# A transformer block on one core: a rewritten order for the first hundred microseconds

## The chip, the cores and the metric

The kernel runs on one core of one Trainium2 chip. The core has five engines that run at the same time and wait for each other through semaphores: TensorE (PE; its weight loads are shown apart as PEld), VectorE (DVE), ScalarE (ACT), GpSimd (POOL) and SyncE (SP), which in this kernel issues nearly all DMAs. The metric is the device time of one execution in microseconds (us). Three runs of the kernel before took 2388.63, 2390.82 and 2393.79 us; the median is 2390.82.

## The reference

The input is four sequences of 4096 rows of 512 values. In order:

```python
x = x + 0.5 * ffn(layernorm(x), weight, bias)
x = x + attention(layernorm(x), qkv_w, qkv_b, rpb, proj_w, proj_b)
x = x + 0.5 * ffn(layernorm(x), weight, bias)
```

`ffn` is one matrix product of 512 by 512. Both operands are first rounded, in blocks of 32 along the inner dimension, to a six-bit floating-point grid with one scale for each block, and scaled back; so the weight, too, has to be quantised before the first product. `attention` has 16 heads of 32; every row sees 13 neighbours, with a bias by relative position, and is followed by an output projection.

## The kernel before, in words

The 16384 rows are 128 tiles of 128 rows; four tiles are a group. Every product is done in float16 with a high and a low half of each operand: `product` (L146) issues twelve matmuls for 512 output columns, low weight half first. All weights lie in one tile `wt`, as 2 halves x 4 chunks of the inner dimension x 2560 columns: 512 each for queries, keys, values and the output projection, and last the FFN weight, from column FO. A weight is worked on in its row layout, 128 rows at a time, and has to be transposed on its way into `wt`.

Work on a tile is cut into stages that run at numbered slots (`begin`, `run_slot`, L162 to L169): a stage issues some instructions, yields how many slots later and at what rank it goes on, and within a slot low ranks are issued first. One tile advances by STEP = 7 slots. Engines execute in the order of issue. The stages are:

- `load` (L174), `moments` and `quantised_norms` (L214, L220): statistics on VectorE, factors on POOL (`factors`, L183), the normalised tile on ScalarE, block maxima on VectorE, a product with the reciprocal on POOL, rounding to fp8 on ScalarE, a product with the scale on POOL, then the high half on ScalarE, the low half on VectorE (`low`, L202) and a DMA transpose into `xT`;
- `first_half` (L281): the FFN product `pmf` on TensorE, its addition to x (L279), the second norm, halves `hln`, and a DMA transpose into `x2`, which holds a group. `add_bias` puts half the FFN bias onto x on POOL (L568);
- `values` (L303): the product `pmv`, its halves `vt`, and a store `vd<-vt`;
- `project_qk` (L353): two products `pmqk` for one head group, which need all four tiles of the row group in `x2`. This is item m. `softmax` (L421) computes scores `ps`, VectorE, POOL and ScalarE work in turn, and transposes the probabilities by DMA, `pT<-p` (L489). `attend` (L492) multiplies with the stored values, which `load_stack` (L398) has loaded back, `vs<-vd`. Then come `project_out` and `second_half`, with the store of the result.

A tile t of k = 7t begins its FFN at slot k + 5 and its values at k + 20; the items begin at slot 38 and then every seven slots.

The setup block (L629 to L873) does three things. It loads the FFN weight `fw` and quantises it by exact steps in four row groups (L745 to L770): VectorE does most of the elementwise work (L752, L756 to L758, L142, L144), POOL the products with the two halves of the scale (L755) and the scaling back (L766), ScalarE the rounding (L762) and the high half (L768), and the sync queue transposes (`wt<-whlf`, L704). It finds powers of two for all weights from sums of squares (`powers`, L670). And it scales the other sixteen weight chunks (`put_scaled`, L781, halves `whl`, L784 and L786, then `wt<-whl`), at slots 2 to 35; `scales` (L795), `attention_bias` (L813, product `pmb`) and `put_table` (L858) belong here. From L779 the code is a written order (`manual_schedule`); what stands before it was put in order by a planner at build time, with its own estimates. The first three tiles are normed there too.

Buffers limit how far engines run apart: three PSUM buffers `ps_m` for products, 23 buffers `x` for tiles.

Of the kernel before, what the change touches and what calls it, by code (L numbers as in the profile page):

```python
# [26 lines left out]
F32 = mybir.dt.float32  # L27
# [10 lines left out]
P = 128  # L38
# [12 lines left out]
QB = 32  # L51
# [13 lines left out]
def macaron_kernel(  # L65
# [70 lines left out]
    def tie_to_lower(t):  # L136

        nc.vector.scalar_tensor_tensor(t, t, BELOW_ONE, t, ALU.mult, ALU.min)  # L142
        ti = t.bitcast(I32)
        nc.vector.tensor_scalar(ti, ti, 1, None, ALU.bitwise_or)  # L144

# [74 lines left out]
    def quantised_norms(slot):  # L220

        tiles, mv = together.pop(slot)
        n = len(tiles)
        rs, nb = factors(slot, "q", mv[0], n)
# [21 lines left out]
        nc.gpsimd.tensor_tensor(yb, yb, bc(r, QB), ALU.mult)  # L246
# [4 lines left out]
        nc.gpsimd.tensor_tensor(  # L251
# [3 lines left out]
        if spare:  # L255
            hl = xp.tile([P, dim], F32, tag="x", name=f"hlq{slot}").bitcast(F16)
            hl = hl.rearrange("p (u s k) -> p u s k", u=1, s=2)
        else:
            hl = hlp.tile([P, 2, 2, dim], F16, tag="hlq", name=f"hlq{slot}")[:, :n]
# [11 lines left out]
    def ffn(t, which):  # L271

        xT = ys.pop(t)
        pm = ps_m.tile([P, dim], F32, tag="mm", name=f"pm{which}_{t}")
        product(
            pm, lambda s, c: xT[:, s, c, :], lambda s, c: wt[:, s, c, FO : FO + dim]
        )
        yield 1, 8
        nc.vector.scalar_tensor_tensor(xs[t], pm, cf, xs[t], ALU.mult, ALU.add)  # L279

    def first_half(t):  # L281

        yield from ffn(t, "f1")
        yield 1, 2
        mv = sm.tile([P, 1, 2], F32, tag="mvn2", name=f"mvn2_{t}")
        statistics(t, "n2", mv[:, 0, :])
        yield 1, 2
        rs, nb = factors(t, "n2", mv)
        yield 1, 2
        y = yp.tile([P, 1, dim], F32, tag="yn2", bufs=1, name=f"yn2_{t}")  # L290
        nc.scalar.activation(y[:, 0], xs[t], AF.Identity, bias=nb, scale=rs)
        hl = hlp.tile([P, 1, 2, dim], F16, tag="hln2", name=f"hln2_{t}")
# [273 lines left out]

    def add_bias(t, b):
        nc.gpsimd.tensor_tensor(xs[t], xs[t], b, ALU.add)  # L568
# [30 lines left out]
    for t in range(NT):  # L599
        k = t * STEP  # L600
        begin(k - 18, one(load, t), 0)
        enlist(k - 10, t, "n1")
        if not 0 < t < EARLY:
            begin(k - 11, one(moments, k - 10, t, "n1"), 1)
        begin(k + F1, first_half(t))
        begin(k + V, values(t))
        begin(k + F1, one(add_bias, t, half_ffn_b), 8)
# [6 lines left out]
    for slot in together:  # L614
        if slot >= EARLY * STEP - 10:
# [13 lines left out]
    with tc.tile_pool(name="setup", bufs=1) as sp, tc.tile_pool(name="scratch", bufs=2) as scr:  # L629
# [10 lines left out]


        rows = {}

        sq = sp.tile([P, 5 * KC], F32, name="sq")
        first = min(slots)
        for slot in range(first, first + EARLY * STEP, STEP):
            run_slot(slot)
        for _ in quantised_norms(-10):
            pass
        chunks = (8, 9, 10, 11, 12, 13, 14, 15, 0, 4, 1, 5, 2, 6, 3, 7)  # L650
        for o in chunks:
# [3 lines left out]
        for o in (*range(4 * KC, 5 * KC), *chunks):  # L655
            src = fw[:, o - 4 * KC, :] if o >= 4 * KC else rows[o]
            junk = scr.tile([P, dim], BF16, tag="junk", name=f"junk{o}")
            nc.scalar.activation(junk, src, AF.Square, accum_out=sq[:, o : o + 1])
        ptb = ps_m.tile([P, 512], F32, tag="mm", name="ptb")
        nc.tensor.transpose(ptb[:, : 3 * KC], b12, ident[: 3 * KC, : 3 * KC])  # L660
        bT = sp.tile([P, 3 * KC], F32, name="bT")
        nc.vector.tensor_copy(bT, ptb[:, : 3 * KC])
        b2 = sp.tile([P, 3 * KC], F32, name="b2")
        nc.vector.scalar_tensor_tensor(b2, bT, 2.0 ** -8, bT, ALU.mult, ALU.mult)
        nc.vector.tensor_tensor(sq[:, : 3 * KC], sq[:, : 3 * KC], b2, ALU.add)
        top5 = sp.tile([P, 5], F32, name="top5")
        up = sp.tile([P, 5], F32, name="up")
        down = sp.tile([P, 5], F32, name="down")

        def powers(lo, hi):  # L670
# [7 lines left out]
            nc.tensor.transpose(ptn[:w, :P], top5[:, lo:hi], ident)  # L678
            most = sp.tile([w, 1], F32, name=f"most{lo}")
            nc.vector.tensor_reduce(most, ptn[:w, :P], AX.X, ALU.max)  # L680
            diag = sp.tile([w, w], F32, name=f"diag{lo}")
            nc.vector.tensor_scalar(diag, ident[:w, :w], most, 2.0, ALU.mult, ALU.mult)
            ones_w = sp.tile([w, P], F32, name=f"ones{lo}")
            nc.gpsimd.memset(ones_w, 1.0)
            pb = ps_m.tile([P, 512], F32, tag="mm", name=f"pb{lo}")
            nc.tensor.matmul(pb[:, :w], ones_w, diag, start=True, stop=True)
            e = sp.tile([P, w], I32, name=f"e{lo}")
            nc.vector.tensor_copy(e.bitcast(F32), pb[:, :w])
            nc.vector.tensor_scalar(e, e, 23, None, ALU.logical_shift_right)
            nc.vector.tensor_scalar(e, e, 131, None, ALU.add)  # L690
            nc.vector.tensor_scalar(e, e, 1, None, ALU.logical_shift_right)
            nc.vector.tensor_scalar(e, e, 97, None, ALU.max)
            u, d = up[:, lo:hi].bitcast(I32), down[:, lo:hi].bitcast(I32)
            nc.vector.tensor_scalar(u, e, -1, 264, ALU.mult, ALU.add)
            nc.vector.tensor_scalar(u, u, 23, None, ALU.logical_shift_left)
            nc.vector.tensor_scalar(d, e, -10, None, ALU.add)
            nc.vector.tensor_scalar(d, d, 23, None, ALU.logical_shift_left)

        powers(4, 5)
# [219 lines left out]
```

## Time and profile before

| | |
|---|---|
| median of three runs | 2390.82 us |
| the profiled execution | 2398.3 us, of them 2396.5 us span |
| TensorE busy | 2285.3 us (95%) |
| VectorE busy | 2020.8 us (84%) |
| GpSimd busy | 1990.2 us (83%) |
| ScalarE busy | 1329.8 us (55%) |
| first FFN product, first q/k projection | at 58.50 us, at 107.18 us |

The page of a profile gives busy times and shares of the span, 40 slices with the busy share in tenths, and the costliest groups of instructions. A line of a timeline reads: start in us, duration in us, engine, line, operation, output <- inputs, shapes, count, and in brackets the idle time of the engine before it and what ended it. "SPq" is the sync queue: its durations are the time of issuing a DMA, and the data land later. A group's mean can mix shapes.

### The profile page before, as it was taken

To read this page: it belongs to the slowest core of one execution; us is meant where nothing else is said; L and a number is where in the kernel's file an instruction comes from. 1 tells how busy PE (TensorE), PEld (TensorE's weight loads), DVE (VectorE), ACT (ScalarE), POOL (GpSimd) and SP (SyncE) were. 2 spreads that over 40 slices of the span, in tenths; PEclk is the share of its full clock that TensorE was granted. 3 is DMA by queue.
4 is the path that set the end of the run, shared out by engine and by line. 5 is a ranking of instruction groups with operands and counts; after the bars stand their busy time and mean duration, and the time that the engine had idled before them with its cause. 6 is when DMAs were issued, how large, how long until landed. Compare 5 with 4: busy or idle time off the path is not lost.

```text
span 2396.5 us, 82360 instructions
## 1 busy us (share of the span) xinstructions
PE 2285.3 (95%) x35539; PEld 1118.5 (47%) x35539; DVE 2020.8 (84%) x3588; ACT 1329.8 (55%) x2080; POOL 1990.2 (83%) x2012
## 2 busy tenths in 40 slices
PE   0799999999999999999999999999999999999998
PEld 0344444444444444444444444444444444444443
DVE  8789888888888888888888888888888878888886
ACT  4466555555555555555555555555555555555542
POOL 5578888888888888888888888888888888888886
PEclk9899999999999999999999999999999999999999
DMA  5789788777777777777777778877777786777773
GB/s 153 143 151 155 159 164 159 159 148 151 150 155 158 158 142 150 148 155 156 164 147 149 148 159 161 156 159 146 150 151 158 158 158 131 149 150 152 137 116 108
DMA packets 925701, 360.59 MB, mean 150 GB/s; under 512 B 718876, under 2 KB 889752, under 8 KB 925336
## 3 DMA queue, kind: packets, MB, share of 16 engines
q1 hardware_dynamic: 924992, 354.79, 74.3%
q8 instruction: 278, 4.55, 0.8%
q10 hardware_dynamic: 344, 0.53, 0.1%
q14 instruction: 87, 0.71, 0.1%
HBM read 110.15 MB, written 67.29 MB: 74 GB/s over the span
## 4 chain that ended last, share of the span: by engine, by line
PE 92%; DVE 4%; issue 1%; DMA 1%; POOL 1%; ACT 1%; SPq 0%; DVEq 0%; POOLq 0%; ACTq 0%
PE pmqk L151 28%; PE pmf L151 26%; PE pmo L151 14%; PE pmv L151 14%; PE ps L437 7%; PE pv L507 3%; DVE fw L756 0%; DMA x<-hln 0%; DVE hlq L204 0%; DVE stn L180 0%; DVE whl L786 0%; DMA fw<-in_L_ffn_weight_dram 0%; DVE sc L239 0%; POOL yq L251 0%; DVE x L279 0%
## 5 line engine op out<-in xcount | busy, mean ns | idle before, releaser
L151 PE MATMUL pmf<-wt,xT 128*128 128x512 f16 x3048 | 703.2, 381 | 12.9 <-DMA xT<-hlq 10.3
L151 PE MATMUL pmqk<-x,wt 128*128 128x512 f16 x3072 | 709.3, 381 | 4.8 <-DMA x<-hln 4.6
L151 PEld LDWEIGHTS <-xT 128*128 128x128 f16 x3048 | 298.8, 98 | 377.1 <-DMA xT<-hlq 12.7
L151 PEld LDWEIGHTS <-wt 128*128 128x128 f16 x3072 | 290.6, 98 | 342.7 <-issue 10.4
L151 PE MATMUL pmo<-wt,ring 128*128 128x512 f16 x1536 | 360.5, 385 | 8.5 <-issue 8.5
L151 PE MATMUL pmv<-wt,x 128*128 128x512 f16 x1536 | 354.1, 380 | 4.9 <-DVE mvn L181 4.9
L246 POOL TENSOR_TENSOR yq<-yq,r 128x1024 f32<-128x1024 f32 (+1 forms) x141 | 246.7, 1750 | 131.1 <-DVE r L244 131.1
L568 POOL TENSOR_TENSOR x<-x,half_ffn_b 128x512 f32<-128x512 f32 x256 | 327.8, 1280 | 0.1
L279 DVE SCALAR_TENSOR_TENSOR x<-pmf,coef,x 128x512 f32<-128x512 f32 x256 | 179.7, 702 | 151.9 <-PE pmf L151 151.6
L534 ACT ACTIVATE ring<-pv 128x510 f16<-128x510 f32 (+8 forms) x224 | 82.6, 415 | 396.6 <-PE pv L507 396.6
L314 ACT CAST vt<-pmv 128x512 f16<-128x512 f32 x128 | 75.1, 587 | 389.2 <-PE pmv L151 389.2
L180 DVE BATCH_NORM_STATS2 stn<-x 128x6 f32<-128x512 f32 x384 | 265.4, 691 | 9.0 <-DMA x<-in_L_attn_x_dram 0.2
L251 POOL TENSOR_TENSOR yq<-q,sc 128x1024 f32<-128x1024 fp8e4 (+1 forms) x141 | 246.9, 1751 | 1.0 <-ACT q L249 1.0
L151 PEld LDWEIGHTS <-x 128*128 128x128 f16 x1536 | 150.7, 98 | 187.6 <-DMA x<-hln 5.4
L377 DVE SCALAR_TENSOR_TENSOR qk<-pmqk,qk_b,qk 128x512 f16<-128x512 f32 x256 | 190.7, 745 | 52.9 <-ACT qk L373 51.8
L151 PEld LDWEIGHTS <-ring 128*128 128x128 f16 x1536 | 141.6, 99 | 173.2 <-issue 19.9
L480 POOL TENSOR_TENSOR sf<-sf,total 128x714 f32<-128x714 f32 (+2 forms) x128 | 178.8, 1397 | 42.8 <-DVE total L478 22.9
L186 POOL TENSOR_SCALAR rsq<-mv 128x2 f32<-128x2 f32 (+1 forms) x141 | 130.0, 922 | 99.3 <-DVE mv L181 96.9
L249 ACT ACTIVATE q<-yq,nudge 128x1024 fp8e4<-128x1024 f32 (+1 forms) x141 | 150.3, 1066 | 112.0 <-POOL yq L246 103.8
L373 ACT ACTIVATE qk<-pmqk,qk_b 128x512 f16<-128x512 f32 x256 | 176.5, 689 | 52.2 <-PE pmqk L151 50.4
L233 ACT ACTIVATE yq<-x,nbq,rsq 128x512 f32<-128x512 f32 x254 | 193.6, 806 | 18.3 <-POOL nbq L192 17.6
L487 POOL TENSOR_TENSOR p<-sf,p 128x714 f16<-128x714 f32 (+2 forms) x128 | 192.8, 1506 | 0.1
(145 smaller groups left out, 3466.3 us busy)
## 6 DMA issues: line engine op xcount, KB each, us to landing
vs<-vd SPq DMA_DIRECT2D x144, 357.0 KB
x<-in_L_attn_x_dram SPq DMA_DIRECT2D x128, 256.0 KB
vd<-vt SPq DMA_DIRECT2D x128, 256.0 KB
out_dram<-x SPq DMA_DIRECT2D x128, 256.0 KB
vs<-vd SPq DMA_DIRECT2D x24, 378.0 KB
vs<-vd SPq DMA_DIRECT2D x24, 315.0 KB
rows<-in_L_attn_qkv_w_dram SPq DMA_DIRECT2D x12, 256.0 KB
xT<-hlq SPq DMA_TRANSPOSE x141
```

What stands on the lines that cost most here:

```text
L151: nc.tensor.matmul(pm, lhs(a, c), rhs(b, c), start=(n == 0), stop=(n == 3 * KC - 1))
L180: nc.vector.bn_stats(st, xs[t])
L233: nc.scalar.activation(y[:, u], xs[t], AF.Identity, bias=nb[:, u : u + 1], scale=rs[:, u : u + 1])
L246: nc.gpsimd.tensor_tensor(yb, yb, bc(r, QB), ALU.mult)
L251: nc.gpsimd.tensor_tensor(yb, q8.rearrange("p u (n q) -> p (u n) q", q=QB), bc(sc, QB), ALU.mult)
L279: nc.vector.scalar_tensor_tensor(xs[t], pm, cf, xs[t], ALU.mult, ALU.add)
L373: nc.scalar.activation(t[:, s, 0, KN:], pms[s], AF.Identity, bias=bias)
L377: nc.vector.scalar_tensor_tensor(t[:, s, 1, KN:], pms[s], bias, t[:, s, 0, KN:], ALU.add, ALU.subtract)
L437: nc.tensor.matmul(ps[rows, u, :sides, w * KN : (w + 1) * KN], t[rows, 0, part, q0 : q0 + QR], t[rows, 1, :sides, k0 : k0 + KN], start=par ...
L480: nc.gpsimd.tensor_tensor(s, s, bc(total[:, :n], KN), ALU.mult)
L487: nc.gpsimd.tensor_tensor(p[:, :n, KN : 2 * KN], s, ph, ALU.subtract)
L568: nc.gpsimd.tensor_tensor(xs[t], xs[t], b, ALU.add)
```

## The change

It concerns the setup block and the slots of the first six tiles; from tile 6 on the stages are the same and stand at the same slots.

1. The written order now begins before the setup's work; the planner orders only what comes ahead of it (the first loads and constants). The order of the setup is written out with generators that are advanced step by step (`run`, `both`).
2. The FFN weight is quantised by VectorE alone apart from ScalarE's rounding: L755 and L766 move from POOL to VectorE. Row groups 0 and 1 are done first, then 2 and 3. The scaled-back weight is transposed by TensorE in 128 by 128 pieces into PSUM; ScalarE copies the high half into `wt` and VectorE subtracts for the low half. The DMA transposes of the FFN weight are gone. For the first two tiles, the two products of `quantised_norms` move to VectorE.
3. `begin_ffn` issues the first 256 columns of the FFN product of tiles 0 and 1, as soon as row groups 0 and 1 are in `wt`; `ffn` then issues the other 256.
4. The first six tiles get slots of their own for norm, FFN and values (N1, FIRST, VALUES), and `first_half` other waits between its steps.
5. The other weights: early chunks are loaded first; values come at slots 6 to 9, the first two items' queries and keys at 15 to 34, the rest at 42 to 51, the output projection at 56 to 67, where they stood at 2 to 35. The bias product moves from slot 28 to 70, the table from 26 to 31.

```diff
@@ quantised_norms
+        mult = nc.vector if slot in N1[:2] else nc.gpsimd
...
-        nc.gpsimd.tensor_tensor(yb, yb, bc(r, QB), ALU.mult)
+        mult.tensor_tensor(yb, yb, bc(r, QB), ALU.mult)
...
@@ ffn, first_half
+    def begin_ffn(t):
+
+        xT, n = ys[t], dim // 2
+        pm = ps_m.tile([P, dim], F32, tag="mm", name=f"pmf1_{t}")
+        product(pm[:, :n], lambda s, c: xT[:, s, c, :], lambda s, c: wt[:, s, c, FO : FO + n])
+        begun[t] = pm, n
...
+        if which == "f1" and t in begun:
+            pm, n = begun.pop(t)
+        else:
+            pm, n = ps_m.tile([P, dim], F32, tag="mm", name=f"pm{which}_{t}"), 0
         product(
-            pm, lambda s, c: xT[:, s, c, :], lambda s, c: wt[:, s, c, FO : FO + dim]
+            pm[:, n:], lambda s, c: xT[:, s, c, :], lambda s, c: wt[:, s, c, FO + n : FO + dim]
         )
-        yield 1, 8
+        yield wait, 8
...
+        soon = t < SOON
+        yield from ffn(t, "f1", (2 if t in begun else 3) if soon else 1)
...
@@ slots
+    N1, FIRST, VALUES = (-3, -2, -1, 6, 9, 17), (5, 6, 11, 20, 23, 30), (17, 21, 25, 33)
+    SOON = len(FIRST)
...
-        begin(k + F1, first_half(t))
-        begin(k + V, values(t))
+        begin(first_slot(t), first_half(t))
+        begin(VALUES[t] if t < len(VALUES) else k + V, values(t))
...
@@ setup
+        ctx.enter_context(tc.manual_schedule())
...
-        chunks = (8, 9, 10, 11, 12, 13, 14, 15, 0, 4, 1, 5, 2, 6, 3, 7)
+        chunks = (8, 9, 10, 11, 0, 4, 1, 5, 2, 6, 3, 7, 12, 13, 14, 15)
+        early = chunks[:6]
...
             nc.vector.tensor_tensor(qh, fwb, per(w_r), ALU.mult)
-            for i, b in enumerate((w_hi, w_lo)):
-                u = large("wu_", f"{o}_{i}")
-                nc.gpsimd.tensor_tensor(u, qh, per(b), ALU.mult)
+            yield
+            for b in (w_hi, w_lo):
+                nc.vector.tensor_tensor(u, qh, per(b), ALU.mult)
+                yield
                 nc.vector.tensor_tensor(fwb, fwb, u, ALU.subtract)
+                yield
...
-            nc.gpsimd.tensor_tensor(fwb, w8, per(w_back), ALU.mult)
-            hl = scr.tile([P, 2, dim], F16, tag="whl", bufs=4, name=f"whlf{o}")
-            nc.scalar.copy(hl[:, 0, :], fw[:, o, :])
-            nc.vector.tensor_tensor(hl[:, 1, :], fw[:, o, :], hl[:, 0, :], ALU.subtract)
-            put_weights(4 * KC + o, hl)
+            nc.vector.tensor_tensor(fwb, w8, per(w_back), ALU.mult)
...
+            for c in range(KC):
+                nc.tensor.transpose(pt[:, c, :], fw[:, o, c * P : (c + 1) * P], ident)
+            h, l = (wt[:, s, :, FO + o * P : FO + (o + 1) * P] for s in (0, 1))
+            nc.scalar.copy(h, pt)
+            yield
+            nc.vector.tensor_tensor(l, pt, h, ALU.subtract)
+            yield
...
+        ready = [quantise(o) for o in range(KC)]
+
+        def both(o, n=1):
+
+            for _ in range(n):
+                run(ready[o])
+                run(small_ones)
+                run(ready[o + 1])
+                run(small_ones)
...
+        both(2)
+        begin_ffn(0)
+        moments(n1_slot(2), 2, "n1")
+        run(norms[2])
+        run(norms[1])
+        squares(*chunks[11:14])
+        both(2)
+        run(norms[2])
+        run(norms[1])
+        begin_ffn(1)
+        squares(*chunks[14:])
+        both(2)
+        both(2)
+        run(norms[2])
+        both(2)
...
-        begin(0, one(scales), 9)
-        for slot, o in zip((2, 4, 5, 6, 10, 13, 16, 19, 21, 23, 25, 27, 29, 31, 33, 35), chunks):
+        begin(5, scales(), 0)
+        begin(6, norms[2], 1)
+        for slot, o in zip((6, 7, 8, 9, 15, 18, 32, 34, 42, 44, 49, 51, 56, 60, 64, 67), chunks):
             begin(slot, put_scaled(o), 9)
-        begin(28, attention_bias(), 9)
-        begin(26, one(put_table), 9)
+        begin(70, attention_bias(), 9)
+        begin(31, one(put_table), 9)
```

## The prediction, made before the changed kernel ran

> **What bounds the kernel now.** I read the page's shares and slices first, then the stretches, then TensorE in order of time, then VectorE and the sync queue (SPq) where TensorE waits.
>
> From the page: shares of the span, and TensorE and its granted clock in 40 slices of 60 us.
> ```profile
> span 2396.5 us, 82360 instructions
> PE 2285.3 (95%) x35539; PEld 1118.5 (47%) x35539; DVE 2020.8 (84%) x3588; ACT 1329.8 (55%) x2080; POOL 1990.2 (83%) x2012
> PE   0799999999999999999999999999999999999998
> ```
> TensorE is full from the third slice on; only the first two slices and the end are not. The answer by stretches (us; then busy time of PE, PEld, DVE, ACT, POOL; clock; DMA share; GB/s) says how full:
> ```profile
> 58.50:107.20 48.70, 33.29 (x109) 12.50 (x110) 35.69 (x63) 22.58 (x35) 24.04 (x37) 0.82 0.74 148
> 118.80:130.40 11.60, 11.60 (x185) 5.72 (x177) 10.95 (x24) 6.32 (x11) 9.01 (x12) 1.00 0.64 106
> 142.00:158.00 16.00, 12.52 (x249) 6.38 (x241) 14.82 (x33) 10.42 (x18) 13.10 (x17) 0.95 1.12 178
> 260.00:2300.00 2040.00, 2021.15 (x32004) 994.36 (x32002) 1737.41 (x3057) 1156.58 (x1782) 1742.68 (x1716) 1.00 0.76 152
> ```
> From 260 to 2300 us TensorE idles 19 us of 2040: a microsecond won or lost earlier arrives at the end whole. TensorE's timeline gives the marks of the head:
> ```profile
> 58.50 5.28 PE L151 MATMUL pmf<-wt,xT-10_160 128*128 128x512 f16 x12 [15.17 <-DMA wt<-whlf]
> ...
> 107.18 5.34 PE L151 MATMUL pmqk<-x,wt 128*128 128x512 f16 x24 [1.01 <-DMA x<-hln]
> 112.36 2.75 PE L151 MATMUL pmf<-wt,xT 128*128 128x512 f16 x12
> 114.95 2.75 PE L151 MATMUL pmv<-wt,x 128*128 128x512 f16 x12
> ```
> First FFN product at 58.50, at half rate (0.43 us a matmul, against 0.216 later); first q/k projection at 107.18, and no gap after it until 154.5. There it waits 3.55 us for a transposed tile, by the sync queue's timeline:
> ```profile
> 133.28 4.59 SPq L489 DMA_TRANSPOSE pT<-p  x1
> 137.97 1.24 SPq L205 DMA_TRANSPOSE xT<-hlq  x1
> 139.31 1.29 SPq L205 DMA_TRANSPOSE x<-hln  x1
> 140.65 2.92 SPq L413 DMA_DIRECT2D vs<-vd  x6
> 143.66 0.52 SPq L316 DMA_DIRECT2D vd<-vt  x1
> 144.22 1.95 SPq L176 DMA_DIRECT2D x<-in_L_attn_x_dram  x1
> 146.28 4.89 SPq L489 DMA_TRANSPOSE pT<-p  x1
> 151.28 2.25 SPq L205 DMA_TRANSPOSE xT<-hlq  x1
> 153.62 1.29 SPq L205 DMA_TRANSPOSE x<-hln  x1
> ```
> From the first probabilities (133.28) to the awaited tile (153.62) the queue issues without a pause, while the DMA share is 1.12. VectorE's timeline, last, has one tensor_tensor with POOL at work and one with POOL idle:
> ```profile
> 26.95 1.53 DVE L756 TENSOR_TENSOR fw<-fw,wu 128x512 f32<-128x512 f32 x1
> 45.61 0.67 DVE L758 TENSOR_TENSOR wq<-wq,wqh 128x512 f32<-128x512 f32 x1
> ```
> At 43 to 46 us such operations start every 0.60 us.
>
> **Part 1, the FFN weight.** POOL loses eight products (L755, 1.37 us) and four (L766, 1.57 us), 17.2 us; VectorE gets them, and POOL is then nearly idle, so I take 0.61 us for each. Per row group that is nine elementwise steps up to the scaling back (5.5) and an integer one (0.40): 5.9, for four groups 23.6. Ahead of the last transposes VectorE also has two subtractions from PSUM (1.3), norms 0 and 1 (statistics 0.82, maxima and reciprocal 1.1, two products 1.22, subtraction 0.61: 3.75 each, the products being POOL's before), half of norm 2 (1.9), four maxima of the weight (2.6), some forty small ones (6.0) and waits for the loads (0.9). Sum 43.8; it begins at 6.04 as before, so ends at 49.8. Then TensorE's order holds the path: the transposes of the third and fourth group stand behind the begun product of tile 1. Its low half ends 4.3 us before 49.8 (two tie steps 1.2, two integer ones 0.8, the maxima 1.1, two scalings 1.2), at 45.5; it lands 3.2 later (the chain's row at 55.18), 48.7; twelve half-width matmuls at half rate 2.6, 51.3; eight transposes at 0.37 (L678's row), 54.3; ScalarE's copy 0.6, the last subtractions about 1.1: weight ready at 56.0, against 58.5. The sixteen transposes (5.9 us) lie in TensorE's idle time; four DMA transposes leave the sync queue.
>
> Bounds: 53.2 if the begun product holds nothing up; 58.6 if the transposes take twice the row. I take 56.0, from the single-transpose row.
>
> [...]
>
> **Part 2, up to the first q/k projection.** VectorE was busy 35.7 of the 48.7 us before. Taken away: five of thirteen scaled-weight subtractions (L786, 0.74: 3.7), the bias product's two (1.4). Added: the rest of the powers and the scales (2.2), the sixth tile's update and statistics (1.5), two low halves (1.2). That leaves 35.5. Its waits were 13.0, 7.1 of them for the first cold product, which now only has half its columns to go while VectorE has the powers. But norms 3 and 4 now stand ahead of tile 0's normalisation on POOL and ScalarE, and VectorE's step on tile 0's values stands behind a product that starts cold: some 2.5 us. Waits 5.9 + 2.5, taken as 8.5 (bounds 6 and 13). Projection at 56.0 + 35.5 + 8.5 = 100.0: 7.2 us earlier.
>
> **Part 3, products moved across it.** f1 of tile 5 and values of tile 3 leave the stretch between the first projection and the first scores (10.45 us, 107.18 to 117.63). TensorE would save 5.2, but the scores wait for VectorE to fold in the second half (0.9 after the projection in the trace) with a queue as long as before: 6.6 instead of 10.45, 3.9 won. Sum 11.1.
>
> **Part 4, weights later.** Three subtractions (2.2 us) now stand on VectorE between the first scores and the first probabilities, which had 0.65 us idle in an item of 11.6: 1.55 lost, sum 9.5. On the sync queue the probabilities' transpose, a wait on POOL, holds all behind it; two weight transposes now come between it and the awaited tile, 1.25 us each: 2.5 lost, sum 7.0. Bounds 0 (the 4.89 us of the second pT against 3.2 elsewhere is a backlog that may shrink) and 5.8 (three issues took 8.66 us at 59.30). I keep the issue's own 1.25. The last three of the sixteen go where the DMA share is 0.44, and cost nothing if it stays there. Each late weight also takes ScalarE 0.72 (L784), busy 6.3 of 11.6 there. In the head the loads of tiles 3 and 4 go behind the last weight rows on the sync queue, some 25 us in by its earlier pace (0.6 each), long before norms 3 and 4 read them at 56: nothing.
>
> **Part 5, the bias product** (twelve matmuls) lay in idle time at 92 to 100 us; now it comes at a time when TensorE has no gap: 2.6 lost. Moving half_ffn_b's scaling to ScalarE, tiles into the x pool and constants costs nothing: ScalarE is busy 55%, and the tiles only keep buffers apart.
>
> Sum: 7.2 + 3.9 - 1.55 - 2.5 - 2.6 = 4.4 us. The profiled execution took 2398.3 us (1.8 outside its span), so 2393.9 by its own time; it stands 7.5 above the median of the runs, 2390.8, and carried over that gives 2386.4. A change under 0.2% (4.8 us) can hardly be told from none.
>
> **Rivals.**
> (a) The sync queue does not hold the tile: the backlog shrinks as stack loads start earlier, part 4's 2.5 falls away, and VectorE waits only 6.0. Gain 9.4: 2381.4, down to 2376. For: hln of tile 7 is done on VectorE at 147.5, six us before it is issued. Against: the queue had no pause from 133.28.
> (b) Later weights cost the slow issue (2.9 us) in the full queue, and four of them stand in it: 11.6 instead of 2.5, so 2395.5, slower. It ends the gain from 1.7 us each. For: DMA share 1.12 there. Against: only two lie between the first pT and the awaited tile.
> (c) VectorE's elementwise steps stay at L756's mean, 1.13 us. Thirty-six of them at 0.52 more delay the weight by 18.7: 2405, half of it 2395.8. It ends the gain from 0.12 us each. Against: 0.67 wherever POOL idles.
> (d) The begun halves buy nothing, because the second halves wait for the weight anyway; 2.6 of the 7.1 us of waits return: 2389.0, inside the main case.
>
> **How the numbers follow.** Main case with (d), 0.55, own range 2381 to 2391: half beyond 0.2%, half within. (a) 0.22, all faster. (b) 0.11, two thirds slower. (c) 0.12, nearly all slower. Faster 0.27 + 0.22 = 0.49; same 0.26 + 0.05 = 0.31; slower 0.20. The range runs from 2378, inside (a), to 2398, past (b) and the half of (c); some 0.15 is left out.
>
> **What would show it.** L756's mean near 0.67; last weight subtraction near 56 and the first full-width FFN product some us later; first pmqk near 100; ps within 7 us of it; the wait for x<-hln before the fifth pmqk grown from 3.55 to about 8; pmb without a gap around it. Wrong, if L756's successors stay above 0.8, if pmqk comes after 105, or if that wait is gone.

## The result, and the profile after

The changed kernel took 2425.19 us (median of 2420.62 to 2426.82) where the kernel before took 2389.73 beside it: ratio 1.0153, 95% interval 1.0116 to 1.0189. It is 35 us slower; the forecast was 4.4 us faster. The profiled execution after took 2424.44 us, the one before 2398.3, longer than each of its four timed runs; the spans differ by 26.2 us.

The page of after, answering the first lines of before:

```profile
span 2422.7 us, 82405 instructions
...
PE 2296.4 (95%) x35579; PEld 1124.6 (46%) x35579; DVE 2015.9 (83%) x3615; ACT 1327.2 (55%) x2081; POOL 1972.1 (81%) x1995
...
PE   2789999999999999999999999999999999999997
...
q1 hardware_dynamic: 920768, 353.74, 78.0%
```

The first two slices are fuller, as meant. The last line is the data queue: packets, MB, share of 16 engines. The same line of before, and below it that of the queue of kind "instruction", which is needed further down:

```profile
q1 hardware_dynamic: 924992, 354.79, 74.3%
q8 instruction: 278, 4.55, 0.8%
```

Fewer bytes now take more of the DMA engines. By stretches of after (columns as in the prediction):

```profile
52.89:104.21 51.32, 33.69 (x121) 14.14 (x121) 34.62 (x75) 20.83 (x31) 29.11 (x43) 0.74 0.56 108
260.00:2300.00 2040.00, 2006.98 (x31522) 984.82 (x31521) 1714.28 (x3028) 1142.10 (x1762) 1723.80 (x1696) 1.00 0.81 151
```

From 260 to 2300 us, which the change does not touch, TensorE now idles 33 us where it idled 19, and in the same time does 31,522 matmuls where it did 32,004. So the loss is there, and not in the head. The head is what happens up to some 176 us; TensorE's timeline of after shows it:

```profile
46.38 2.74 PE L141 MATMUL pmf<-wt,xT-2_443 128*128 128x256 f16 x12 [8.15 <-DMA xT-2_443<-hlq-2_431]
48.91 1.79 PE L857 MATMUL ptw<-ident,fw 128*128 128x128 f32 x8
...
52.89 2.34 PE L141 MATMUL pmf<-wt,xT-3_380 128*128 128x256 f16 x12
55.03 2.32 PE L141 MATMUL pmf<-wt,xT-2_443 128*128 128x256 f16 x12
64.90 5.30 PE L141 MATMUL pmf<-wt,xT-1_592 128*128 128x512 f16 x12 [7.55 <-DMA xT-1_592<-hlq-1_567]
74.66 5.30 PE L141 MATMUL pmv<-wt,x 128*128 128x512 f16 x12 [4.46 <-DMA x<-hln]
...
99.12 5.30 PE L141 MATMUL pmv<-wt,x 128*128 128x512 f16 x12 [4.11 <-DMA x<-hln]
104.21 5.51 PE L141 MATMUL pmqk<-x,wt 128*128 128x512 f16 x24
111.29 1.21 PE L450 MATMUL ps<-qk 32*32 32x84 f16 x128 [1.56 <-DVE qk L390]
```

The first q/k projection comes 3.0 us earlier than before (107.18), the first scores 6.3 (117.63). Then the gain shrinks: 2.8 at the first probabilities, 2.35 at the fifth projection (155.72 for 158.07). From one place on, all five engines execute the same instructions in the same order in both kernels to the end; TensorE reaches it (matmul 34,332 from the last) at 176.2 us before and 175.7 after. I call what follows the steady part. The head's rewriting has won half a microsecond there, and the steady part takes 2243.2 us instead of 2216.3. Its instructions being equal, something beside the order of work must have changed.

The list of waits by cause shows what TensorE waits for. Of before (us in total, times, longest), the lines with "issue", in which nothing that the profile shows is awaited:

```profile
PE ps L437 <- issue: 9.3, 7, 3.4
PE pmo L151 <- issue: 8.5, 4, 4.7
...
PE pv L507 <- issue: 1.2, 1, 1.2
...
PE pmqk L151 <- issue: 0.2, 1, 0.2
```

Of after:

```profile
PE pmo L141 <- issue: 17.4, 8, 3.5
...
PE pmqk L141 <- issue: 9.2, 6, 3.6
...
PE ps L450 <- issue: 7.2, 3, 5.3
PE pv L520 <- issue: 7.1, 9, 2.0
```

The sums are 19.2 and 40.9 us: 21.7 of the 26.2. In the trace each of these gaps in the steady part ends 1.2 to 1.8 us after the end of a 16,384-byte packet of the queue of kind "instruction". There are 278 of them, as many as there are whole blocks of 256 in the 71,196 rows that the trace of before lists for TensorE (71,274 after; a weight load and a matmul are a row each). Counted in these rows, all of these gaps over 0.7 us in the two executions stand at the same place within a block of 256, row 193 or 194. So TensorE waits for its own instructions, which come in blocks of 256 rows through a queue that the profile lists beside that of the data. Of the 278 blocks only 10 before and 17 after cost a gap of over 0.7 us, but with the shorter ones that is 19 and 41 us.

Some 3 of the other 4.5 us go with the clock: the granted clock is 0.50 for 3.4 or 6.8 us at several of the longer gaps, and over the steady part these stretches are worth 16.6 us of full clock after, 13.5 before.

Why would the blocks be later? The trace's packets between 300 and 2300 us (my own means over the packet records, ns):

| packets | before | after |
|---|---|---|
| 512 bytes: loads of the value stacks, vs<-vd | 43.0 | 50.9 |
| 1024 bytes: stores vd<-vt | 56.4 | 61.2 |
| 256 bytes: transposes | 24.6 | 25.5 |

The packets of the first two lines are as many in both executions (138,108 and 32,768), the transposes' 0.6% fewer; what has changed is where their tiles lie. The change moves three small tiles, `up`, `down` and `vb`, from a pool that ends with the setup into the constants, which stand ahead of all later buffers: 96 bytes per partition with rounding. Every later tile's first byte moves by 96. Counted within 256 bytes, the stacks `vs` began at 0 and now begin at 96, `x` too; `hl`, `vt` and `ring` at 128, now at 224.

### The profile page after: what moved, and what is told of

The parts are those of the page before. It is cut to its first block, busy times and chain, and to the rows that moved or that the text cites. A ratio compares the mean times of both kernels' runs of the same rounds, so it can differ in the third digit from the quotient of the medians.

```text
span 2422.7 us, 82405 instructions
## 1 busy us (share of the span) xinstructions
PE 2296.4 (95%) x35579; PEld 1124.6 (46%) x35579; DVE 2015.9 (83%) x3615; ACT 1327.2 (55%) x2081; POOL 1972.1 (81%) x1995
## 4 chain that ended last, share of the span: by engine, by line
PE 89%; DVE 5%; issue 3%; POOL 2%; DMA 1%; ACT 1%; SPq 0%; POOLq 0%; DVEq 0%; ACTq 0%
PE pmqk L141 27%; PE pmf L141 25%; PE pmo L141 14%; PE pmv L141 13%; PE ps L450 6%; PE pv L520 3%; DVE stn L170 1%; DVE whl L1003 0%; DVE qk L390 0%; DVE x L283 0%; POOL yq L238 0%; DMA x<-hln 0%; DVE sc L231 0%; DVE hlq L194 0%; DMA fw<-in_L_ffn_weight_dram 0%
## 5 line engine op out<-in xcount | busy, mean ns | idle before, releaser
L141 PEld LDWEIGHTS <-ring 128*128 128x128 f16 x1536 | 141.2, 98 | 177.7 <-issue 24.6
L225 ACT ACTIVATE yq<-x,nbq,rsq 128x512 f32<-128x512 f32 x253 | 192.3, 803 | 25.2 <-POOL nbq L182 24.5
```

Source lines behind the costliest of these rows:

```text
L141: nc.tensor.matmul(pm, lhs(a, c), rhs(b, c), start=(n == 0), stop=(n == 3 * KC - 1))
L225: nc.scalar.activation(y[:, u], xs[t], AF.Identity, bias=nb[:, u : u + 1], scale=rs[:, u : u + 1])
```

## Experiments: the placement

The first theory is that this shift is the loss; the rival is that something in the new order is.

**e1**, the kernel before with 96 unused bytes in the constants:

```diff
     halo = const.tile([P, KC, 2, 2, KN], F16, name="halo")
+    const.tile([P, 24], F32, name="gap")
```

> The kernel before with one unused tile of 96 bytes per partition behind the constants; no instruction changes, but every buffer behind it stands 96 bytes higher, as the three small constants of the change put it. Theory A (placement: stack loads and other DMAs run slower because the buffers no longer begin at a multiple of 256 bytes, and TensorE's instruction fetches wait behind them): about +20 us over the kernel before, mean time of the 512-byte packets about 51 ns instead of 43. Rival B (TensorE's instruction stream, 40 matmuls longer, meets the transfers at other moments) and rival C (the order of the later weights leaves the sync queue in another rhythm): no difference, within 0.2%.

**e2**, the changed kernel with 160 unused bytes there, so that its shift is 256 and every tile is back at its old place within 256 (same line, `[P, 40]`).

> The changed kernel with an unused tile of 160 bytes more, so that all buffers behind the constants stand 256 bytes higher than before and begin where they did modulo 256. Theory A: the 20 us or so that are lost after 200 us come back; what is left is the change of the head itself, so between 5 us faster and 8 us slower than the kernel before, and 512-byte packets at 43 ns. Rivals B and C: as slow as the changed kernel, +1.5%.

**e3**, the changed kernel with the 160 bytes in the pool of the attention tiles only: `vs`, `pT`, `p`, `ring` are back, `x`, `hl`, `vt` stay 96 off.

> The changed kernel with the 160 bytes ahead of the buffers of the attention stage alone (ring, p, qk, sf, pT, stack): these begin where they did modulo 256, the x tiles, hl, xT, x2 and vt remain 96 off. Theory A with the stack loads as the cause: nearly all of e2's gain. Theory A with the x tiles (loads and stores of 2048 bytes) or the transposed tiles as the cause: at most a quarter of it. Rivals B and C: no gain.

**e4**, the kernel before moved by 128 bytes (`[P, 32]`).

> The kernel before with 128 unused bytes behind the constants: x, pT and the stack now begin at 128 modulo 256, and hl, xT, x2, vt and ring, which began at 128, at 0. If what counts is a start at a multiple of 256 for the stack's 512-byte rows: about +20 us. If it is a multiple of 64 or 128: no loss. If the transposed tiles count more than the stack: a gain of 5 to 15 us. Rivals B and C: no difference.

**e5**, the kernel before moved by 256 bytes (`[P, 64]`), as a control.

> The kernel before with 256 unused bytes in the constants, so that every later buffer moves by 256 bytes and none changes its place within 256. The theory of the placement says no change: within 0.2% of the kernel before, 512-byte packets at 43 to 44 ns, TensorE waiting for its instructions for some 25 us between 160 and 2330 us. If the shift as such cost (another bank, another distance to the constants), it would be over 10 us slower, as the shift of 96 bytes was.

**e11**, the kernel before with a pool of 96 bytes just ahead of the pool of the stacks, which is the last: nothing else moves.

> The kernel before with the stacks of values alone moved by 96 bytes, everything else in its place. If the stack loads are the whole cost of the placement, 512-byte packets take 50 to 51 ns, 1024-byte ones some 61, the 256-byte ones of the transposes stay at 24.6, and the kernel is 25 to 35 us slower, as with all moved. If the probabilities and the other buffers count too, it is 10 to 20 us slower.

**e8**, the kernel before with 128 unused bytes ahead of the pools of `hl` and of `pT`: all that a DMA touches begins at 0 within 256.

> The kernel before with two unused gaps of 128 bytes, after which every buffer that a DMA reads or writes begins at a multiple of 256 bytes. The theory of the placement says that the 256-byte packets of the transposes fall from 24.6 to some 21 ns, as they did where the normalised copies lay at such a place by chance, with the 512-byte packets kept at 43 ns: the DMA engines are freed by some 2% of the span, and the kernel is 0 to 10 us faster than before. If the transposes' packets are not on the way of the instructions, no change.

Ratios are to the kernel before on the same chip (median 2384.62 us beside e1 to e4, 2392.18 beside e5 and e8, 2384.82 beside e11):

| run | vs at (of 256) | time, us | ratio (95%) | 512 B, ns | 256 B, ns |
|---|---|---|---|---|---|
| e1 before, all + 96 | 96 | 2420.83 | 1.0138 (1.0101 to 1.0174) | 50.7 | 25.6 |
| e11 before, only vs + 96 | 96 | 2426.27 | 1.0146 (1.0120 to 1.0173) | 50.5 | 25.1 |
| e4 before, all + 128 | 128 | 2414.38 | 1.0104 (1.0075 to 1.0134) | 47.8 | 21.3 |
| e5 before, all + 256 | 0 | 2395.30 | 1.0014 (0.9995 to 1.0032) | 42.8 | 24.7 |
| e8 before, all at 0 | 0 | 2394.47 | 1.0019 (1.0002 to 1.0036) | 42.6 | 21.0 |
| e2 after, all + 256 | 0 | 2397.10 | 1.0047 (1.0031 to 1.0063) | 43.5 | 24.5 |
| e3 after, attention tiles back | 0 | 2397.57 | 1.0047 (1.0031 to 1.0062) | 43.4 | 24.8 |

The placement is shown both ways: put on the kernel before it costs 1.4%, taken from the changed one it gives back 1.06 of the 1.53%. The tile is named too: with the stacks alone moved (e11) the whole loss is there, with only the attention tiles put back (e3) the whole recovery. The distance as such does nothing (e5). Several expected sizes were missed: e1 came 36 us slower where about 20 was said, e4 30 for 20, e11 41 for 25 to 35; e2 stayed 12 us slower where at most 8 was expected, which the next section is about; e5's waits for instructions were 13 us for 25; and e8 was not faster.

TensorE's waits in e11, a kernel whose instructions are those of before:

```profile
PE pmo L151 <- issue: 13.9, 4, 4.5
PE ps L437 <- issue: 9.9, 6, 3.0
...
PE pv L507 <- issue: 8.7, 8, 2.2
...
PE pmqk L151 <- issue: 3.9, 4, 1.7
```

36.4 us instead of 19.2, and nothing else in its waits has grown by more than 3: the late blocks make up 17.2 of the 17.7 us between the two profiled spans, with 7.5 ns more per stack packet. These two executions are e11's shortest and a long one of before; the 41 us between the medians have no trace of their own. Over all the profiles the waits with "issue" are 10 to 23 us where the stacks begin at 0, 30 in e4, and 35 to 41 in e1, e11 and after. The 1024-byte stores slow down in e11 too (61.1 ns), though their tile has not moved, and are back at 56.9 in e3, where it is still 96 off: their time goes with the stacks' place, not with their own.

By size of packet: the stacks' 512 bytes took 43 ns at a multiple of 256, 51 at 96 past one and 47.8 at 128; the transposes' 256 bytes fall from 24.6 to 21.0 in e8 and 21.3 in e4, where `hlq`, `hln`, `xT` and `x2` came to lie at 0. Both sizes were fastest where their tiles lay at 0; why, the runs don't show.

e8 corrects the obvious next step, that the load of the DMA engines is what counts. The data queue's line of e8:

```profile
q1 hardware_dynamic: 924992, 354.79, 68.4%
```

and of e4:

```profile
q1 hardware_dynamic: 924992, 354.79, 70.3%
```

Both load the engines less than before (74.3%); one is no faster, the other 1.0% slower. What counts, it seems, is what is under way when a block is asked for. I took the time from 2 us before each gap of over 0.7 us until the late block started, and summed the packets in it: the 512-byte stack loads fill 66 to 80% of the 16 engines' time there in the kernel before (two profiles, before and e5), 86% in the changed kernel realigned (e17 below), against 17% over the whole steady part; the transposes 11 to 22%, and nearly nothing in e17, against 45%. The blocks that come in time are the control: of those with stack loads in under 20% of the engines' time in the 3 us ahead of them, 1 of 197 was late (a gap of over 0.3 us) before and 2 of 195 in e17; of those with over 80%, 9 of 28 and 10 of 26. So most late blocks are those that fall on a stack load, though not every block that does is late. That fits the stack packets costing time and the transposes' not. Whether the fetch is queued behind them, and how, the trace doesn't show.

## Experiments: the rest, and where the instruction stream is cut

The realigned changed kernel was still 0.47% slower. Its steady part has the instructions of before and begins no later (174.2 us in e2), and yet the whole takes longer. My second theory was that the rows by which TensorE's stream is longer, which I took to be 52, put its cuts every 256 rows at other instructions; the rival was the order of the head (later weights). I tried it with tiny products of 32 x 32 x 32 at the start of the setup, which write nothing that is used:

```diff
+        zero = sp.tile([32, 64], F16, name="zero")
+        nc.vector.memset(zero, 0.0)
+        spare = ps_m.tile([P, 512], F32, tag="mm", name="spare")
+        for _ in range(26):
+            nc.tensor.matmul(spare[:32, :32], zero[:, :32], zero[:, 32:], start=True, stop=True)
```

**e6** is that on the kernel before (each product is two rows), **e12** the same again on another chip.

> The kernel before with 26 tiny products (32 x 32 x 32) at its start, which make TensorE's stream 52 instructions longer, as the change makes it (71,123 for 71,071), with no buffer moved. The theory that the 0.47% which remain with the buffers realigned come from where the instruction stream is cut into its blocks of 256 rows says 5 to 12 us slower than before, with more TensorE time lost to late instructions. The theory that they come from the order of the head itself (later weights, the queue of the transposes) says within 3 us of the kernel before; the products themselves take under 1.5 us and lie in the wait for the first loads.

> The kernel before with 26 tiny products at its start, which was 0.29% faster on the chip where it ran, a second time. If where the instruction stream is cut counts, 4 to 10 us faster than before again, with the steady part at 170 us instead of 175. If that was one chip's, within 0.2%.

**e7** is the realigned changed kernel with 102 of them, meant to make up a whole block against before.

> The changed kernel with its buffers realigned to 256 bytes (as in the run that moved them by 256) and 102 tiny products more at its start, so that its stream is 256 instructions longer than that of the kernel before and its blocks are cut at the same instructions as there. The theory of the blocks says that the remaining 0.47% go: 2378 to 2388 us, between 6 us faster and 2 us slower than before. The theory of the head's order says that nothing moves: 2394 to 2400 us, 0.47% slower.

e6 was not slower but faster, 0.9971 (0.9955 to 0.9987), and missed both expectations; e12 did not repeat the gain, 0.9992 (0.9973 to 1.0011); e7 came to 1.0011 (0.9990 to 1.0032), which fits neither of its two. The places of the gaps tell more. They recur at the same matmuls of the steady part in the runs of one stream, and stand multiples of 128 matmuls (256 rows) apart, with a slow drift from the semaphore rows between them: before at 671, 1311, 8980, 28155; in e2 and e9 both at 504, 1528, 4851, 11242, 18145, 27860. Modulo 128, the early ones are at 31 before, at 5 to 6 in e6 and e12 (26 less), at 120 to 121 in the changed kernel, at 17 in e7. I call this number the cut of a run. So the cut is real, and my 52 was wrong: the trace has 78 rows more after than before, 39 products' worth, so that e6 had not the changed kernel's cut, nor e7 that of before. The next runs have, to within a matmul.

**e9** is e2 again, beside **e10**, the same with the later weights and the bias product at about their old slots:

```diff
-        for slot, o in zip((6, 7, 8, 9, 15, 18, 32, 34, 42, 44, 49, 51, 56, 60, 64, 67), chunks):
+        for slot, o in zip((6, 7, 8, 9, 13, 15, 18, 19, 21, 23, 25, 27, 29, 31, 33, 35), chunks):
...
-        begin(70, attention_bias(), 9)
+        begin(37, attention_bias(), 9)
```

> The changed kernel with every later buffer moved to the places within 256 bytes that it had before, a second time, with the other three on one chip. From 175 us on, every engine has the same instructions in the same order as the kernel before. If the remaining 0.47% belong to the change, it is 6 to 15 us slower than before again. If they were that chip's (the kernel before moved by 256 bytes was 0.14% slower than before on the other, the changed one with longer stream 0.11%), it is within 0.2%.

> The changed kernel, buffers realigned, with the ten later weights and the bias product put back to about the slots that they had before. The reading of the head says that the 3 to 4 us won up to the first scores are lost between 130 and 175 us, where these weights now stand; without them there, the steady part begins 2 to 4 us earlier than with them, and the time falls by as much. The prediction's part 4 says the same (4 us back, less what VectorE loses ahead of the first projection). If the later weights cost nothing, the steady part begins where it did, at 173 to 175 us, or later.

e9: 2400.36 us, 1.0049 (1.0031 to 1.0066): the rest is not that of one chip. e10: 2398.09 us, 1.0041 (1.0026 to 1.0056); its steady part began at 170.9 us instead of e9's 175.6, more than the 2 to 4 us expected, but the times differ only by 2.3 us and their intervals overlap.

**e13** gives the kernel before the cut of after (38 products), **e14** the changed one the cut of before (90), **e15** that of e6 (115), **e16** is e15 with e10's early weights.

> The kernel before with 38 tiny products at its start, which put the cuts of TensorE's instruction stream (every 256 rows) at the same instructions of the steady part as in the changed kernel. If the cut is the cause of the remaining 0.47%, it is 6 to 14 us slower than before, with waits for instructions at matmul 4851, 11242, 18145 and 27860 of the steady part, as in the changed kernel. If not, within 4 us of before.

> The changed kernel, buffers realigned, with 90 tiny products at its start, which put the cuts where they are in the kernel before. If the cut is the cause, it is within 4 us of the kernel before, with waits at matmuls 671, 1311, 8980 and 28155. If it is something else in the change, it stays 0.4 to 0.5% slower (9 to 13 us).

> The same with 115 products: the cuts of the run of the kernel before with 26 products more, which was 0.29% faster than before on one chip and 0.08% on another. If the cut is the cause: from 7 us faster than before to 1 us slower. If not, 0.4 to 0.5% slower.

> The same as the run with 115 products, and the ten later weights and the bias product back at their earlier slots. If the 3 to 5 us by which that began the steady part earlier are real and the cut is the rest, it is 4 to 9 us faster than the kernel before. If either falls, within 4 us of it or slower.

**e17** and **e18** are e2 and e15 once more, on one chip.

> The changed kernel with its buffers realigned, beside the next on one chip. If the cut is the cause of the remaining 0.47%: 0.2 to 0.5% slower than before, a steady part of 2215 to 2224 us with the waits at matmuls 4851, 11242, 18145 and 27860. If the slower time was that of two chips, within 0.2%.

> The same with 115 tiny products at the start and nothing else different. If the cut is the cause: 8 to 18 us faster than the run without them on this chip, a steady part of 2200 to 2210 us. If not, within 4 us of it.

All with aligned stacks, sorted by cut; the two columns before the time are from the profiled executions, in us. The ratio is to the kernel before on the same chip (medians 2384.62 beside e2 and e3, 2392.18 beside e5 to e8, 2384.82 beside e9 to e12, 2391.15 beside e13 to e16, 2393.48 beside e17 and e18):

| cut | run | steady part begins | takes | time | ratio (95%) |
|---|---|---|---|---|---|
| 121 | e2 after | 174.2 | 2215.6 | 2397.10 | 1.0047 (1.0031 to 1.0063) |
| 121 | e9 after | 175.6 | 2223.3 | 2400.36 | 1.0049 (1.0031 to 1.0066) |
| 121 | e17 after | 174.3 | 2219.3 | 2397.82 | 1.0023 (1.0007 to 1.0040) |
| 121 | e3 after, attention tiles back | 172.7 | 2220.6 | 2397.57 | 1.0047 (1.0031 to 1.0062) |
| 121 | e10 after, early weights | 170.9 | 2214.8 | 2398.09 | 1.0041 (1.0026 to 1.0056) |
| 121 | e13 before + 38 | 168.5 | 2218.1 | 2389.43 | 0.9997 (0.9983 to 1.0011) |
| 31 | before | 176.2 | 2216.3 | | |
| 31 | e5 before | 174.7 | 2205.9 | 2395.30 | 1.0014 (0.9995 to 1.0032) |
| 31 | e8 before | 173.6 | 2215.3 | 2394.47 | 1.0019 (1.0002 to 1.0036) |
| 31 | e14 after + 90 | 173.2 | 2212.2 | 2389.17 | 0.9990 (0.9975 to 1.0004) |
| 17 | e7 after + 102 | 175.1 | 2216.7 | 2394.24 | 1.0011 (0.9990 to 1.0032) |
| 6 | e6 before + 26 | 170.2 | 2204.5 | 2384.69 | 0.9971 (0.9955 to 0.9987) |
| 6 | e12 before + 26 | 168.8 | 2206.9 | 2384.25 | 0.9992 (0.9973 to 1.0011) |
| 6 | e15 after + 115 | 173.2 | 2201.9 | 2388.03 | 0.9992 (0.9976 to 1.0007) |
| 6 | e18 after + 115 | 174.6 | 2200.0 | 2386.44 | 0.9974 (0.9958 to 0.9990) |
| 6 | e16 after + 115, early weights | 170.9 | 2201.9 | 2381.87 | 0.9968 (0.9954 to 0.9983) |

The length of the steady part goes with the cut and not with the kernel: 2215 to 2223 us at 121, 2200 to 2207 at 6, in both, and 2206 to 2216 at 31. These columns are one execution each, and some are far from their run's median: e5, e10, e15 and e18 were profiled in their shortest, 6 to 9 us below it. If each difference is put on the steady part, it is 2215 to 2222 at 121, 2208 to 2215 at 31 and 2205 to 2210 at 6. The direct pair is e17 and e18, one chip, one kernel, 115 idle products apart: 2397.82 and 2386.44, 11.4 us, in the 8 to 18 expected. The trace shows it instruction by instruction. TensorE's timeline of e17:

```profile
264.37 1.03 PE L142 MATMUL pmqk<-x,wt 128*128 128x512 f16 x4
268.21 3.30 PE L142 MATMUL pmqk<-x,wt 128*128 128x512 f16 x8 [2.81 <-issue]
...
477.43 0.82 PE L142 MATMUL pmo<-wt,ring 128*128 128x512 f16 x3
480.89 2.10 PE L142 MATMUL pmo<-wt,ring 128*128 128x512 f16 x9 [2.65 <-issue]
```

A product of twelve matmuls breaks after the fourth and another after the third, with nothing awaited, and these are the gaps at matmuls 1528 and 4851. The eight matmuls after the first gap take 3.30 us: the granted clock is 0.50 from 267.7 to 271.1 us and 1.00 on either side. The first product in e18:

```profile
262.51 2.75 PE L142 MATMUL pmqk<-x,wt 128*128 128x512 f16 x12
265.19 0.20 PE L521 MATMUL pv<-pT,vs 126*32 126x30 f16 x3
265.97 0.70 PE L521 MATMUL pv<-pT,vs 126*32 126x30 f16 x69 [0.58 <-issue]
```

The same product is whole, and the cut, now among the attention products, costs 0.58. All of e18's waits for instructions, behind those of e17:

```profile
PE pmo L142 <- issue: 12.4, 9, 2.9
...
PE pmqk L142 <- issue: 5.4, 3, 2.8
PE ps L451 <- issue: 4.9, 2, 3.7
```

```profile
PE ps L451 <- issue: 3.2, 2, 1.9
PE pmo L142 <- issue: 3.2, 3, 1.4
...
PE pv L521 <- issue: 2.3, 3, 1.2
...
PE pmqk L142 <- issue: 1.0, 2, 0.5
```

9.9 us with a 0.2 not shown, against 22.7 in e17; the stretches of halved clock in the steady part are worth another 12.8 us in e17 and 4.5 in e18.

e13 missed its expectation of 6 to 14 us slower. Its gaps came where expected (4852, 11243, 18146 and 27861 of the steady part), which took 2218 us; but it began at 168.5 us. In the head of before there is no wait with "issue"; what e13 is spared is most of the wait of 3.55 us for `x<-hln` (0.72 is left) and the half rate of the product behind it (5.23 us for 2.75), 5.3 us in all, and there is a wait for instructions of 0.75 us at 142.7 instead. e6 and e12 show the same exchange (1.61 and 1.49 us), and so do e10 and e16, the changed kernel with early weights. So the head changes as well; whether through the cut or otherwise, the runs don't show. The table tells about the new order, too: at cut 121 it begins the steady part 4 to 7 us later than the old one (e13; e10, with early weights, 2), at cut 6 3 to 6 us later, at 31 it is 0.4 to 3 earlier. The head's gain over the kernel before was within what a few idle products move. e14 was as fast as expected, but has two of the four gaps expected, at 1309 (0.42 us) and 28153; e15 and e17 came as expected.

e16 beats both kernels: 9 us below before (0.9968, 0.9954 to 0.9983), and 6.2 below e15 on its chip. Its early weights begin the steady part 2.3 us sooner; the rest of the 6.2 the traces don't explain.

Open: the kernel before itself had medians from 2384.6 to 2393.5 us on the chips here, with the same stream; the cause of that was not tried, and ratios near 0.2% should be read with it in mind. The record shows that the granted clock goes with it: its mean over the timed runs is 0.9925 and 0.9924 where the median is lowest, 0.9912 where it is highest, which by itself makes, as an estimate, 3.1 of the 8.9 us (0.13% of the time). In e2, e9 and e17 it is 0.0034 to 0.0040 below that of before on the same chip. The clock is a rival for part of the 0.2 to 0.5%, or the way in which the waits cost time, since several halved stretches begin at gaps; nothing here separates the two.

## Why the prediction was wrong, step by step

**Part 1, the FFN weight: right.** VectorE's tally was to end at 49.8. Its timeline of after has the last scaling and the last subtractions:

```profile
47.13 2.86 DVE L846 TENSOR_TENSOR fw<-w,w_back 128x512 f32<-128x512 fp8e4 x2 [0.56 <-ACT w L841]
...
51.06 1.27 DVE L861 TENSOR_TENSOR wt<-ptw,wt 128x512 f16<-128x512 f32 x2
```

The scaling ends at 49.99. VectorE's groups of after from 20 to 52 us (count, busy us, mean ns, idle before) give the elementwise steps, for which 0.61 was taken:

```profile
L846 DVE TENSOR_TENSOR fw<-w,w_back 128x512 f32<-128x512 fp8e4 x4 | 4.2, 1076 | 0.6 <-ACT w L841 0.6
L827 DVE TENSOR_TENSOR fw<-fw,wu 128x512 f32<-128x512 f32 x5 | 3.2, 682 | 0.0
...
L831 DVE TENSOR_TENSOR wq<-wq,wqh 128x512 f32<-128x512 f32 x4 | 2.6, 676 | 0.0
```

The elementwise steps took 0.68 instead of 0.61 and the scaling back, L846, 1.08: some 4 us more for the thirty-six. That the tally still ended where it was said is luck: the smaller terms were too large by as much. The weight was ready at 52.3 instead of 56.0: the begun product of tile 1 came at 46.38 (48.7 said), and eight transposes took 1.79 us, not 3.0: in a row each takes 0.22, the single one that I took as their row 0.37. (By the terms listed, the upper bound for transposes at twice the row would have been 59.0, not 58.6.) Rival (c) fell. The second halves took 2.34 and 2.32 us for 12 x 256 columns, where twelve 512-column matmuls at full rate take 2.75: 1.9 us more than at full rate, at a granted clock of 0.62 (52.89 to 57.40 us), a loss for which my sum had no term. TensorE had done eight transposes and then idled for 1.79 us shortly before these halves; whether the clock followed either, no run here tells.

**Part 2, the first projection: the size of the waits was wrong.** It came at 104.21, not 100.0, although the weight was early: 51.3 us from the second halves instead of 44. (In e14 and e15, the same order behind idle products, it came at 99.35 and 99.55; in the other runs of this order at 101.85 to 104.0.) VectorE's work was as summed (34.62 for 35.5), its waits 16.7 instead of 8.5, beyond my bound of 13. TensorE ran at a granted clock of 0.74 in this stretch (0.82 before) and waited 7.55, 4.46 and 4.11 us for single tiles, and three products ran at half rate, 5.30 us. 8.4 of VectorE's 16.7 us are three waits for ScalarE's half of the values (`vt`), behind products that came late and cold; I had priced one cold product, at 2.5.

**Part 3, the scores: right.** 7.1 us after the projection, 6.6 said, 10.45 before.

**Part 4, the later weights: right in kind, wrong in place.** The sync queue's timeline of after:

```profile
130.52 3.08 SPq L502 DMA_TRANSPOSE pT<-p  x1
133.69 1.26 SPq L738 DMA_TRANSPOSE wt<-whl  x1
...
142.20 2.89 SPq L738 DMA_TRANSPOSE wt<-whl  x1
...
145.82 4.33 SPq L502 DMA_TRANSPOSE pT<-p  x1
150.25 1.25 SPq L195 DMA_TRANSPOSE xT<-hlq  x1
151.59 2.06 SPq L195 DMA_TRANSPOSE x<-hln  x1
```

Two weight transposes stand before the awaited tile, as said, at 4.15 us for 2.5. The loss between the scores and the first probabilities was 3.6 us, not 1.55, that between the probabilities and the tile 0.4, not 2.5: 4.0 for 4.05 in sum, which is luck. The wait for the tile grew to 6.03 (8 said). e10 and e16 put the weights and the bias product back, and their steady part began 4.7 and 2.3 us sooner, where parts 4 and 5 make 6.65.

**Part 5.** The bias product took 2.75 us without a gap at 173.13, as said. But "tiles into the x pool and constants costs nothing ... the tiles only keep buffers apart" is the step that failed: three constants, 96 bytes together, cost some 25 us (1.0153 against e2's 1.0047), because they shift the stacks from a multiple of 256 bytes to 96 past one (43.0 to 50.9 ns a packet). No row of before could have priced it; but the diff shows that the change adds to a pool ahead of all others, and a term that no row bounds should have widened the range upwards.

**The sum's frame** failed as well. "A microsecond won or lost earlier arrives at the end whole" holds only if the steady part keeps its length, and with 40 matmuls more in the head it does not: the cut of the instruction stream is worth up to 11 us (e17 and e18), more than the whole forecast gain. The 19 us that TensorE idled there before had been taken as given.

The rivals all argued about the head, and none is what decided. (a) fell: the queue did hold the tile. (b)'s price, 2.9 us an issue, held for one of the two. (c) fell with part 1 (0.68 and 1.08 us a step for its 1.13, and the weight early). (d), that the begun halves buy nothing, was not tried.

## What to carry to other kernels

Before moving a tile into a pool that lies ahead of others, work out where each DMA's tile then begins within 256 bytes, and try a pad that keeps the old places; here the stack loads' 512-byte packets went from 43 to 51 ns with 96 bytes, and 160 unused bytes were worth 25 us. Where a full engine shows idle time with "issue", see whether it ends just behind an instruction packet (here 1.2 to 1.8 us), and at which instructions it stands: if at the same ones in every run, a few idle instructions ahead may move it; here 115 idle products saved 11.4 us (e18 against e17), more than the 4.4 forecast for the change, so compare two orders at the same cut. A lower share of the DMA engines was no gain by itself (e8: 68.4% for 74.3%, and no faster): what counted here, it seems, was which transfers lie where something short is awaited.

## What the runs showed of the hardware that I had not expected

- A 512-byte packet of the stack loads took 43 ns when the stacks began at a multiple of 256 bytes (before), 47.8 at 128 past one (e4), 51 at 96 past one (after); a 256-byte packet of the transposes 21.0 with their tiles at 0 (e8), 24.6 before.
- TensorE's instructions came as DMA packets in the midst of the data's: 278 blocks of 16 KB, 1.1 us each (before and after), and 10 us (e18) to 41 us (after) of waiting for them in one execution of 2.4 ms, depending on the placement of one tile and on the number of instructions ahead.
- Most of these waits recurred at the same instructions in the runs of one stream, from chip to chip (504, 1528, 4851, 11242, 18145 and 27860 in e2 and e9), so they look like a property of the code's order, though in the steady part that order is the same in both kernels.
- In e17 a gap of 2.81 us ended in a stretch of 3.4 us at a granted clock of 0.50, so that it cost more than its length.
